# A graph layer with routed experts: first groups of 256 nodes, four row buffers, head steps placed later

## The chip, the cores and the metric

The kernel runs on one core of a Trainium2 chip. A core has a matrix engine (PE, with its weight loads shown apart as PEld), a vector engine (DVE), a scalar engine (ACT), a general engine (POOL, which here makes the descriptors of indirect transfers) and a queue engine (SP, which here issues the plain transfers). Each engine runs its own instructions strictly in the order in which they were written and waits at semaphores for the others. The metric is the device time of one execution in microseconds (us), given as the median of several runs.

## The reference

One layer over 6250 nodes of 256 features and 200000 edges:

```python
xn = layernorm(x)
# edges: w = sigmoid(relu(xn[dst] @ W1 + b1) @ W2 + b2)
num = segment_sum(xn[dst] * w, src); den = segment_sum(w, src)
gnn = where(den > 0, num / max(den, 1e-12), 0)
# heads: 8 heads of 32 channels; k and v are xn normalised per head, kv = k^T v / N
mix = xn @ kv (per head) + xn
x = x + gnn + mix
# experts: softmax of a small router over layernorm(x), the best 2 of 6,
# each expert three 256x256 products with relu between; weighted sum of the two
out = x + experts(layernorm(x))
```

The weight w depends only on the node at the far end of an edge, so it is computed once per node. The indices dst are uneven: low node numbers occur far more often.

## The kernel before, in words

The 6250 nodes are 49 tiles of 128 rows (the last has 106). Two tiles are a block (SB = 2) and four tiles a group (GT = 4); so there are 25 blocks and 13 groups.

**Node rows.** Each node gets a row of three bf16 terms of (w·xn, w, 1), 774 values, which is stored in DRAM (`y_rows`). The first 1024 nodes' rows also stay on the chip (`yh`).

**Sorting.** The edges are cut into pieces of 65536 and sorted by src. Two pieces (a and c) are "cold": for each tile of src nodes, windows of 128 sorted edges are gathered from `y_rows` by an indirect transfer (line 902) and summed by a product with a one-hot matrix (line 933, three matmuls for one gather). There are 1176 such gathers, and we count time by them: "gather 144" is the place in PE's order behind 144 × 3 matmuls of line 933. The third piece (b) is "hot": it holds only dst below 768, so its edges are counted into matrices by one-hot products (line 1101, fed by DVE's lines 1092 and 1094) and multiplied with `yh` (line 1120). A remainder of 3392 edges ("few") is gathered at line 526 and added by an indirect transfer into a DRAM table (line 548), whose rows are read back tile by tile (`tb`, line 1112). The sort is a merge network on DVE (lines 263, 278, 279) with transposes on PE (line 308).

**Heads.** `head_squares` (lines 665 to 701) and `heads` (703 to 756) build kv. Per group: two matmuls for the deviations (683), squares on ACT (685), sums by head (690), a square root on ACT (696), two small DVE steps (698, 699); then per pair of tiles four matmuls into `dv` (715), a DVE product `z` (721) and matmuls that accumulate kv (733).

**Experts.** `Work` walks over the groups in two lines of work. `to_sums` adds the heads' output to x (1145), then the hot counts and the cold sums of each block (`hot_sums`, 1107). `to_experts` runs the experts of a group once `before_experts` (layer norm, router, gates) is through: matmuls with 512 moving columns at line 1285 and with 256 at line 1302.

**What sets the order.** All engines' orders are written by a planner in the program. In the sort stage several lines of work are generators that yield a pair (busy, wait) of assumed nanoseconds; `run` resumes whichever is due on an assumed clock, and one gather step is placed after each 4100 assumed ns while the few edges last, then after each 1600. From there on a loop places one gather step, then as much other work as a credit allows: the credit grows by (work left − 150000 ns) / (gather steps left). Its clock `now` goes on by 336 ns per gather step (TERMS × BFNS) and by what the placed work is assumed to take; a step of `before_experts` is placed when that clock has reached its due time. A gather buffer (18 of them) comes free when PE has used it, 10 gathers are issued ahead of the step that uses them, and the tail of 150000 assumed ns is what remains behind the last gather.

Of the kernel before, what the change touches and what calls it, by code (L numbers as in the profile page):

```python
# [17 lines left out]
P = 128  # L18
# [31 lines left out]
def kernel(  # L50
# [614 lines left out]
    def head_squares():  # L665


        def load(g):
            if g < len(groups):
                _, t0, nt, rows, r = groups[g]  # L670
                xts[g] = hw.tile([P, GT, CB, P], FP, name="xt", bufs=3)
                nc.sync.dma_start(xts[g][:, :nt, :, :r], xnT_d[t0 : t0 + nt, :, :, :r].rearrange("t p c n -> p t c n"))

        load(0)
        yield 0, 3000
        for g, t0, nt, rows, r in groups:
            while len(xts) > 2:
                yield 0, 1000
            load(g + 1)
            sqs = []  # L680
            for c in range(CB):
                dev = sq_ps.tile([P, GT * P], FP, name="turn")
                nc.tensor.matmul(dev[:, :rows], centre, xts[g][:, :nt, c, :r], start=True, stop=True)  # L683
                sqs.append(hw.tile([P, GT * P], FP, name=f"sq{c}", bufs=1))
                nc.scalar.activation(sqs[c][:, :rows], dev[:, :rows], AF.Square)
            yield 0, 4000
            sums = sq_ps.tile([P, GT * P], FP, name="turn")[:, : GT * CB * HB4]
            for c in range(CB):
# [7 lines left out]
            nc.scalar.activation(some, sums[:r, : nt * CB * HB4], AF.Sqrt, scale=1.0 / (HC - 1))  # L696
            yield 0, 3000
            nc.vector.tensor_scalar(some, some, EPS, None, op0=ALU.add)
            nc.vector.reciprocal(some, some)
            hsqs[g] = hsq.rearrange("p (t h) -> p t h", h=HB4)  # L700
            yield 300, 0

    def heads():
# [3 lines left out]
        for g, t0, nt, rows, r in groups:  # L707
# [3 lines left out]
            for j0 in range(0, nt, 2):  # L711
                k = min(2, nt - j0)
                for j in range(k):
                    for c in range(CB):
# [1 line left out]
                            dv[:r, (j * CB + c) * P : (j * CB + c + 1) * P], xt[:, j0 + j, c, :r], centre,  # L716
                            start=True, stop=True,
                        )
                yield 0, 2600
                z = zs[j0 // 2]  # L720
                nc.vector.tensor_tensor(
                    z[:r, : k * CB, :P].rearrange("p b (h c) -> p b h c", c=HC),
# [297 lines left out]
        return u, xT  # L1020

    nodes, kept = {}, {}
    last_group = len(groups) - 1

    def load(g):
        _, t0, nt, rows, r = groups[g]
        nodes[g] = node_load(nt, r, x[t0 * P : t0 * P + rows], xnT_d[t0 : t0 + nt])


# [27 lines left out]


    F32NS, BFNS = 1.67, 112.0
    hot_wt = {}  # L1060

    def hot_counts(blk):
# [41 lines left out]
            yield BFNS, 300.0  # L1104
        return cn

    def hot_sums(blk, u):
# [219 lines left out]
    class Work:  # L1327
# [3 lines left out]
        def __init__(self):  # L1331
            self.now, self.due, self.left = 0.0, 0.0, ALL
            self.sums, self.late, self.chain = self.to_sums(), self.to_experts(), []
            self.terms, self.ready, self.begun, self.ended = -1, -1, -1, -1
            self.time, self.landed = [0.0, 0.0], 0.0
            hot_wt[0] = hot_load(0)

        def next_load(self):

# [3 lines left out]
                self.landed = self.now + 10000.0  # L1343

        def to_sums(self):
            for g, (_, t0, nt, rows, r) in enumerate(groups):
# [4 lines left out]
                self.terms = g  # L1351
                self.next_load()
                for blk in range(t0 // SB, -(-(t0 + nt) // SB)):
                    while min(NTILE, (blk + 1) * SB) - 1 not in cold_edges.sums:
                        yield None
                    yield from hot_sums(blk, u)
                while self.ended < g - 2:
                    yield None
                kept[g] = []
                self.chain.append((g, before_experts(u, nt, rows, r, kept[g])))  # L1360

        def to_experts(self):
            for g, (_, t0, nt, rows, r) in enumerate(groups):
                while self.ready < g:
                    yield None

# [5 lines left out]
                    yield took, took * SHARE  # L1372
                self.ended = g

        def spend(self, took):

            self.now += took
            self.left -= took
            while self.chain and self.now >= self.due:
                g, steps = self.chain[0]  # L1380
                try:
                    self.due = self.now + next(steps)
                except StopIteration:
                    self.chain.pop(0)
                    self.ready = g
# [18 lines left out]
    with tc.manual_schedule(engines=ORDERED):  # L1404
        work = Work()
        credit = 0.0
        while cold_edges.done < len(steps_c):
# [15 lines left out]


    bad = const.tile([P, 1], I32, name="bad")
# [127 lines left out]
```

## Time and profile before

| | |
|---|---|
| median of 3 runs | 2050.33 us (2047.11 to 2052.64) |
| profiled execution, its own time | 2332.55 us |
| its span | 2330.6 us |
| granted PE clock, mean | 0.884 |
| busy: PE, DVE, ACT, POOL | 1817.9, 1255.5, 653.1, 1209.0 us |
| gathers of line 902 | 1176, 1127.0 us busy, 958 ns each |

The profiled execution is 282 us longer than the median. A profile is one execution with the recorder on; its parts are compared with each other and with its own time. In a row of waits, "A <- B" says that A stood idle until B was done. "remote" or "another core or an unknown queue" is an event for which the records name no instruction, and "issue" a wait that they don't explain. Busy times of PE are of a pipeline, so a busy PE isn't one at its peak. A matmul of fp32 operands stands as two records in the profile (the heads and the experts), one of bf16 operands as one (lines 933, 1101 and 1120).

### The profile page before, as it was taken

How to read it: one execution, taken by the hardware profiler on the slowest of the kernel's cores; microseconds unless marked ns; L12 is line 12 of the kernel's file. 1: busy time of each engine (PE TensorE's matmuls, PEld its weight loads, DVE VectorE, ACT ScalarE, POOL GpSimd, SP SyncE). 2: the span in 40 equal slices, each digit the busy share in tenths (PEclk: the TensorE clock that was granted, in tenths of full speed). 3: DMA queues.
4: the chain of work that ended last, by engine and by line, in shares of the span. 5: the costliest groups of instructions: out<-in, count | busy, mean ns of one | idle time of the engine just before them, and what ended most of it. 6: DMA issues, size and time to landing. Idle time of an engine off the chain costs nothing.

```text
span 2330.6 us, 30207 instructions
## 1 busy us (share of the span) xinstructions
PE 1817.9 (78%) x9491; PEld 1181.1 (51%) x9491; DVE 1255.5 (54%) x5004; ACT 653.1 (28%) x1438; POOL 1209.0 (52%) x1243
## 2 busy tenths in 40 slices
PE   1663697434566989989889888998989888889997
PEld 0341475323343555555555555555555555556555
DVE  8899565763654646445464445544545445554431
ACT  5674485731011212112121211212112121121332
POOL 0004666646564566666666666666666666663000
PEclk9665798756787999999999999999999999999999
DMA  8744557436444455555555554555555555553000
GB/s 249 213 165 91 116 139 220 130 91 177 119 133 129 126 137 166 142 169 135 137 167 140 168 139 135 164 139 167 139 141 157 142 160 141 140 163 81 15 10 12
DMA packets 163693, 320.57 MB, mean 138 GB/s; under 512 B 31407, under 2 KB 104406, under 8 KB 163526
## 3 DMA queue, kind: packets, MB, share of 16 engines
q0 software_dynamic: 80800, 241.85, 39.1%
q1 hardware_dynamic: 77262, 76.15, 10.6%
q10 hardware_dynamic: 5464, 0.58, 0.3%
q8 instruction: 76, 1.25, 0.2%
q14 instruction: 91, 0.75, 0.1%
HBM read 285.06 MB, written 33.39 MB: 137 GB/s over the span
## 4 chain that ended last, share of the span: by engine, by line
PE 59%; DVE 17%; another core or an unknown queue 8%; issue 7%; ACT 4%; DMA 3%; SPq 1%; POOL 0%; ACTq 0%; DVEq 0%; POOLq 0%
PE px L1285 20%; PE pu L933 14%; PE px L1302 9%; PE ph L1101 4%; PE ph L1120 4%; DVE k_cb L278 2%; DVE k_cb L279 1%; DVE fr L1094 1%; DVE to L1092 1%; DMA xs<-in_x_dram 1%; DVE k_a L278 1%; PE px L1180 1%; PE turn L683 1%; DVE k_a L279 1%
## 5 line engine op out<-in xcount | busy, mean ns | idle before, releaser
L902 POOL DMA_INDIRECT gt<-y_rows,dsts x1176 | 1127.0, 958 | 676.2 <-issue 236.5
L933 PE MATMUL pu<-gt,hot 128*128 128x258 bf16 x3528 | 601.5, 288 | 23.1 <-issue 11.7
L933 PEld LDWEIGHTS <-hot 128*128 128x128 bf16 x3528 | 358.9, 103 | 384.3 <-issue 301.8
L1294 ACT ACTIVATE h<-px,eb_t 128x512 f32<-128x512 f32 (+1 forms) x312 | 205.8, 662 | 546.3 <-PE pu L933 233.2
L1285 PE MATMUL px<-fT,ew_t 128*128 128x512 f32 (+1 forms) x624 | 317.1, 604 | 4.2 <-issue 4.1
L1302 PE MATMUL px<-ew_t,h 128*128 128x256 f32 (+1 forms) x1176 | 309.1, 391 | 3.2 <-ACT h L1294 1.6
L1285 PE MATMUL px<-h,ew_t 128*128 128x512 f32 (+1 forms) x624 | 304.7, 583 | 1.7 <-issue 1.6
L1094 DVE TENSOR_SCALAR fr<-count,rdl 128x128 bf16<-128x128 bf16 x884 | 227.8, 273 | 88.8 <-PE ph L1101 40.7
L1311 DVE SCALAR_TENSOR_TENSOR acc<-px,gate,acc 128x256 f32<-128x256 f32 (+1 forms) x294 | 128.4, 477 | 265.8 <-PE px L1302 128.6
L916 DVE TENSOR_SCALAR hot<-count,loc 128x128 bf16<-128x128 bf16 x1056 | 238.9, 269 | 52.1 <-PE pu L933 25.6
L1101 PE MATMUL ph<-to,fr 128*128 128x256 bf16 x884 | 191.2, 287 | 77.1 <-DVE fr L1094 33.8
L1302 PEld LDWEIGHTS px<-ew_t,h 128*128 128x128 f32 (+1 forms) x1176 | 210.5, 196 | 34.7 <-issue 10.1
L1092 DVE TENSOR_SCALAR to<-count,hloc 128x256 bf16<-128x256 bf16 x612 | 183.5, 302 | 31.4 <-PE ph L1101 19.6
L1120 PE MATMUL ph<-yh,cn 128*128 128x258 bf16 x882 | 139.4, 283 | 34.3 <-issue 16.4
L1103 ACT CAST cn<-ph 128x256 bf16<-128x256 f32 x150 | 54.6, 373 | 362.0 <-PE ph L1101 191.1
L1101 PEld LDWEIGHTS <-fr 128*128 128x128 bf16 x884 | 88.6, 100 | 113.0 <-DVE fr L1094 53.8
L526 POOL DMA_INDIRECT gt<-y_rows,dst_c x27 | 30.4, 1127 | 198.4 <-DVE k_a L279 190.5
L1120 PEld LDWEIGHTS <-cn 128*128 128x128 bf16 x882 | 88.1, 100 | 63.4 <-issue 48.4
L1285 PEld LDWEIGHTS px<-fT,ew_t 128*128 128x128 f32 x624 | 102.1, 202 | 28.6 <-issue 20.5
L1285 PEld LDWEIGHTS px<-h,ew_t 128*128 128x128 f32 x624 | 98.3, 194 | 31.6 <-issue 27.2
L1130 DVE TENSOR_TENSOR cs<-ph,cs 128x258 f32<-128x258 f32 x49 | 20.9, 427 | 149.3 <-PE pu L933 66.2
L1148 DVE TENSOR_TENSOR u<-ph,u 128x256 f32<-128x256 f32 (+1 forms) x49 | 20.3, 421 | 105.8 <-PE pu L933 40.8
(239 smaller groups left out, 1818.8 us busy)
## 6 DMA issues: line engine op xcount, KB each, us to landing
gt<-y_rows,dsts POOLq DMA_INDIRECT x1176
xs<-in_x_dram SPq DMA_DIRECT2D x24, 512.0 KB
y_rows<-ys SPq DMA_DIRECT2D x10, 774.0 KB
table<-zero SPq DMA_DIRECT2D x50, 129.0 KB
tb<-table SPq DMA_DIRECT2D x49, 129.0 KB
xnT_d<-xnT SPq DMA_DIRECT2D x12, 512.0 KB
xt<-xnT_d SPq DMA_DIRECT2D x12, 512.0 KB
u<-in_x_dram SPq DMA_DIRECT2D x12, 512.0 KB
```

What stands on the lines that cost most here:

```text
L278: nc.vector.tensor_tensor(lo, a, b, op=ALU.min)
L902: nc.gpsimd.indirect_dma_start(out=gt.rearrange("p k w -> p (k w)"), out_offset=None, in_=y_rows, in_offset=bass.IndirectOffsetOnAxis(ap=d ...
L916: nc.vector.tensor_scalar(hot1, count[:, half * P : (half + 1) * P], loc[:, j : j + 1], None, op0=ALU.is_equal)
L933: nc.tensor.matmul(self.pu, hot1, gt[:, k], start=(start and k == 0), stop=(stop and k == TERMS - 1))
L1092: nc.vector.tensor_scalar(made[j1], count, loc[:, j1 : j1 + 1], None, op0=ALU.is_equal)
L1094: nc.vector.tensor_scalar(fr, count[:, :P], rdl[:, d1, j1 : j1 + 1], None, op0=ALU.is_equal)
L1101: nc.tensor.matmul(pa, matrices[i], made[j], start=(j == j0), stop=(j == j1 - 1))
L1120: nc.tensor.matmul(pu[:, :W], cn[:, d, s * P : (s + 1) * P], yh[:, d, k], start=(d == 0 and k == 0), stop=(d == HOT - 1 and k == TERMS - 1),)
L1285: nc.tensor.matmul(ph[:, :rows], w[:, e, c, f * P : (f + 1) * P], ins[:, c, :rows], start=(c == 0), stop=(c == CB - 1),)
L1294: nc.scalar.activation(h[:, f, :rows], ph[:, :rows], AF.Relu, bias=bc)
L1302: nc.tensor.matmul(po[:r, j - j0], h2[:, c, j * P : j * P + r], ew_t[2][:, e, c, :], start=(c == 0), stop=(c == CB - 1),)
L1311: nc.vector.scalar_tensor_tensor(acc[:r, j, :], po[:r, j - j0], gate[:r, j, e : e + 1], acc[:r, j, :], op0=ALU.mult, op1=ALU.add)
```

## The change

1. Three assumed waits of the heads' generators grow by 2000 ns each (4000 to 6000, 3000 to 5000, 2600 to 4600), so that later steps stand further behind what they read.
2. The expert groups are no longer the groups of the earlier stages: the first four tiles make two groups of two tiles, then follow groups of four; 14 groups in place of 13.
3. The rows of the table (`tb`) get four buffers in place of two.
4. The planner's clock goes on where no work could be placed: by GATHER − 336 = 914 ns per gather step that found none, and by 100 ns where the loop couldn't step. Such time isn't taken from the work that is left (`filled`).
5. The first block's hot counts wait for ten gather steps after the loop's begin (`listed`).

```diff
-            yield 0, 4000
+            yield 0, 6000
...
-            yield 0, 3000
+            yield 0, 5000
...
-                yield 0, 2600
+                yield 0, 4600
...
+    def expert_groups():
+        t0 = 0
+        while t0 < NTILE:
+            nt = min(SB if t0 < GT else GT, NTILE - t0)
+            rows = min(nt * P, N - t0 * P)
...
+            yield t0, nt, rows, min(P, rows)
+            t0 += nt
...
+    GATHER = 1250.0
...
-        tbs = {t: op1.tile([P, W], FP, name="tb") for t in tiles}
+        tbs = {t: op1.tile([P, W], FP, name="tb", bufs=4) for t in tiles}
...
-            add_sums(u[:, t % GT], cs, t, r)
+            add_sums(u[:, t - t0], cs, t, r)
...
+            self.listed = cold_edges.done + 10
...
-                    while min(NTILE, (blk + 1) * SB) - 1 not in cold_edges.sums:
+                    while min(NTILE, (blk + 1) * SB) - 1 not in cold_edges.sums or cold_edges.done < self.listed:
...
-        def spend(self, took):
+        def spend(self, took, filled=True):
             self.now += took
-            self.left -= took
+            self.left -= took * filled
...
             else:
                 credit = max(credit, 1000.0)
+                work.spend(100.0, False)
             while credit > 0:
                 took = work.step()
                 if took is None:
+                    work.spend(GATHER - TERMS * BFNS, False)
                     credit = 0.0
                     break
...
             if work.step() is None:
-                work.spend(500.0)
+                work.spend(500.0, False)
```

What it does to the order, read from both programs' instruction lists, where each matmul counts once: the heads' last matmul (733) stands at gather 64 in place of 30; the sort's last transpose at gather 119 in place of 116; the first expert matmul at gather 174 in place of 222. The hot counts begin at gather 144 in both. Between gathers 144 and 288 stand 96 expert matmuls of 256 columns (line 1285) in place of 36 of 512, 48 of line 1302 in place of 24, and 156 of line 1120 in place of 180; between 288 and the last gather 428 in place of 440 of line 1285, 414 in place of 440 of line 1302, and 672 in place of 648 of line 1120. Behind the last gather the work is the same but for two matmuls of line 1302.

More of the change, by code (lines that the diff above doesn't have):

```diff
@@ L1022 @@
     nodes, kept = {}, {}
-    last_group = len(groups) - 1
+    def expert_groups():
[3 more added lines that the diff above has]
+            rows = min(nt * P, N - t0 * P)
+            assert rows % P == 0 or nt == 1, "the rows that don't fill a tile make a group of their own"
+            yield t0, nt, rows, min(P, rows)
+            t0 += nt
+    parts = list(expert_groups())
+    last_group = len(parts) - 1
     def load(g):
-        _, t0, nt, rows, r = groups[g]
+        t0, nt, rows, r = parts[g]
         nodes[g] = node_load(nt, r, x[t0 * P : t0 * P + rows], xnT_d[t0 : t0 + nt])
@@ L1105, in hot_counts, with hot_sums @@
         return cn
-    def hot_sums(blk, u):
+    def hot_sums(blk, u, t0):
         tiles = range(blk * SB, min(NTILE, (blk + 1) * SB))
-        tbs = {t: op1.tile([P, W], FP, name="tb") for t in tiles}
+        tbs = {t: op1.tile([P, W], FP, name="tb", bufs=4) for t in tiles}
         for t, tb in tbs.items():
@@ L1345, in to_sums @@
         def to_sums(self):
-            for g, (_, t0, nt, rows, r) in enumerate(groups):
+            for g, (t0, nt, rows, r) in enumerate(parts):
                 while g not in nodes or self.now < self.landed:
@@ L1353, in to_sums @@
                 for blk in range(t0 // SB, -(-(t0 + nt) // SB)):
-                    while min(NTILE, (blk + 1) * SB) - 1 not in cold_edges.sums:
+                    while min(NTILE, (blk + 1) * SB) - 1 not in cold_edges.sums or cold_edges.done < self.listed:
                         yield None
-                    yield from hot_sums(blk, u)
+                    yield from hot_sums(blk, u, t0)
                 while self.ended < g - 2:
@@ L1362, in to_experts @@
         def to_experts(self):
-            for g, (_, t0, nt, rows, r) in enumerate(groups):
+            for g, (t0, nt, rows, r) in enumerate(parts):
                 while self.ready < g:
```

## The prediction

> **What bounds the kernel now.** I cut the span at events of the trace: the first and the last `z` of the heads (246.3 and 396.1 us), the last step of the sort (555.5), gather 144 (591.0), gather 288 (834.3), and the last gather's matmul (2144.5). In the table of stretches the columns are length, busy time of PE, PEld, DVE, ACT and POOL, granted PE clock, share of DMA, GB/s.
>
> ```profile
> 246.30:396.10 149.80, 117.26 (x781) 96.75 (x780) 77.67 (x155) 90.07 (x246) 92.56 (x78) 0.86 0.65 167
> 396.10:555.50 159.40, 70.71 (x395) 50.35 (x394) 101.56 (x216) 82.75 (x230) 93.86 (x93) 0.68 0.44 120
> ...
> 591.00:834.30 243.30, 173.75 (x998) 110.66 (x996) 128.60 (x636) 33.86 (x75) 135.83 (x143) 0.83 0.47 128
> 834.30:2144.50 1310.20, 1161.60 (x6182) 738.66 (x6181) 656.88 (x3076) 250.26 (x486) 827.17 (x871) 0.95 0.54 148
> 2144.50:2330.60 186.10, 169.86 (x679) 107.05 (x677) 57.52 (x211) 55.48 (x103) 0.00 (x0) 0.96 0.04 12
> ```
>
> I call them stages 1 to 5 (1 heads, 2 sort, 3 early blocks, 4 steady part, 5 tail). Stage 4 is PE's: 1161.6 of 1310.2 us busy, at 1.475 us per gather. Stage 3 has fewer experts and yet 1.69 us per gather (243.3 / 144), with PE idle for 69.5 us. Next, who stands in whose way: POOL's waits from stage 3 to 4, then PE's own time line in stage 3.
>
> ```profile
> POOL gt L902 <- issue: 202.5, 646, 1.1
> POOL gt L902 <- PE pu L933: 172.3, 171, 3.2
> POOL gt L902 <- PE ph L1101: 100.5, 94, 6.3
> ```
>
> ```profile
> 605.17 4.84 PE L933 MATMUL pu<-gt,hot 128*128 128x258 bf16 x42
> 609.95 0.24 PE L829 MATMUL pT<-ident,wt_a 24*128 24x24 f32 x1
> 610.12 0.51 PE L933 MATMUL pu<-gt,hot 128*128 128x258 bf16 x3
> 624.91 0.30 PE L829 MATMUL pT<-ident,wt_b 25*128 25x25 f32 x1 [14.28 <-issue]
> ```
>
> An unhindered gather takes 0.95 us and 0.30 us to the next, so 1.25. "issue" is that pause; the other two rows, 273 us, are POOL standing until PE gives a buffer back. The time line has the reverse: PE eats 14 stored gathers in 4.84 us, then stands 14.3 us while POOL issues one per 1.25 us. Both sides wait by turns, so uneven work costs time.
>
> In stages 1 and 2 the chain that ended last runs through DVE's sort steps, PE's head matmuls and transposes. DVE's waits in stage 1:
>
> ```profile
> DVE z L721 <- PE dv L715: 35.0, 12, 9.4
> DVE hsq L698 <- ACT hsq L696: 16.3, 6, 5.2
> DVE z L721 <- remote: 7.5, 1, 7.5
> ```
>
> DVE is idle for 72.1 of 149.8 us, mostly at a `z` or a root that isn't ready, and the sort's steps stand behind it in its order. Prices come from these groups (count, busy, mean ns):
>
> ```profile
> L902 POOL DMA_INDIRECT gt<-y_rows,dsts x1176 | 1127.0, 958 | 676.2 <-issue 236.5 <-PE pu L933 219.5 <-PE ph L1101 100.5
> L1285 PE MATMUL px<-fT,ew_t 128*128 128x512 f32 x576 | 310.7, 631 | 4.2 <-issue 4.1
> L1302 PE MATMUL px<-ew_t,h 128*128 128x256 f32 x1152 | 303.1, 391 | 3.2 <-ACT h L1294 1.6 <-issue 1.3
> L1285 PE MATMUL px<-h,ew_t 128*128 128x512 f32 x576 | 298.4, 609 | 1.7 <-issue 1.6
> L278 DVE TENSOR_TENSOR k_cb<-k_cb 128x512 f32<-128x512 f32 x90 | 61.6, 684 | 10.0 <-ACT k_cb L309 8.3
> ```
>
> The means hold pauses between unlike instructions; in the tail's unbroken runs 16 records of line 1285 take 6.87 us and 16 of line 1302 take 3.45. So a program's matmul (two records) costs 0.86 us of 512 columns and 0.43 of 256 in a run, 1.24 and 0.78 by the means.
>
> **Part 1, the heads' waits.** No instruction is added, but between the first and the last `z` now stand 138 sort steps in place of 92 (58 in place of 37 pairs of lines 278 and 279), and behind the last one 126 in place of 176. Those 50 steps took from 396.5 to 444.6 us in the trace: 48 us go from stage 2, with the scalar engine's counts and PE's transposes around them. Stage 1 gets 42 × 0.684 us and 4 × 0.445 us = 30.5 us of DVE work. If all of it lies in DVE's 72 us of waits, stage 1 stays as long; if none does, it grows by 30.5 and 17 us remain. But PE's order also brings 34 more gathers into stage 1 (64 for 30): POOL had 92.6 us busy and 78 pauses of 0.30 = 116 us, and 34 × 1.25 = 42 make 158, over the 149.8. So the gain is 17 to 40 us. Less head work in front of the few edges' matmuls helps (PE was busy for 117 us). Moved past on SP: the load of the first group's x now stands in front of the last five loads of `xt`, and it waited 16.3 us for the table's scatters; PE's later head matmuls would stand behind it once. I take **28 us**.
>
> A rule stands against it. The Trainium skill (SBUF — State Buffer, on the shared port pair and its "DVE blocks DMA" trap) says that POOL is locked out of the port for descriptors while DVE runs a copy, cast or tensor_scalar in a two-port mode, so that denser DVE work starves gathers. The rows: a gather took 1.02 us between 400 and 530 us with the sort (74.52 us, 73 of them), 0.94 in the steady part. By the row, 34 moved gathers cost 34 × 0.08 = 3 us, inside the 28; by the rule's worst case each waits a whole 0.68 us step, 23 us, and 5 us of the gain remain. The sort steps are two-input operations that page excepts for writes, so I take the row.
>
> **Part 2, groups of two tiles and the planner's clock.** Stage 3 gets 96 half-width matmuls of line 1285 for 36 full ones: 96 × 0.43 − 36 × 0.86 = +10.6 us (by the means 96 × 0.78 − 36 × 1.24 = +30.4); 24 more of line 1302, +10.4 (+18.8); 24 fewer of line 1120, at 0.115 us in runs, −2.8 (−6.8 by their 283 ns). Together +18 us (+42). PE's idle 69.5 us covers both. Does the stage shorten as well? The hot counts, packed into few gathers while no expert work was ready, now alternate with it from gather 174, not 222. At stage 4's busy share (0.887), 192 us of PE work take 216 us, a gain of 27; by the means 216 us take 243, none. POOL's floor, 144 × 1.25 = 180, doesn't bind. I take **14 us**.
>
> Here a second rule speaks against: The Trainium skill (TensorE: Matmul & The Clock Gate, "Why this matters for your kernels") advises against moving sides under 512, as thin products let the clock fall to half. The runs of line 1302 show half the time for half the columns (0.216 to 0.429 us per record), its mean in mixed order 0.62 of it. That is the difference between 27 and none above; the granted clock of stage 3, 0.83, would rise if the gaps fill. I lean to the runs.
>
> Stage 4 loses 12 matmuls of line 1285, 26 of line 1302 and gains 24 of line 1120: −10.3 − 11.2 + 2.8 = −19 us (−28 by the means, 0 if gathers paced it). PE sets the pace there: **19 us**. The second small group adds a router, gates and two table loads of 1.28 us on ACT, which is idle for 210 us of stage 3, and two transfers on SP; nothing.
>
> **Part 3, four `tb` buffers, `listed`, idle clock.** SP stood 431.8 us for line 1129 of DVE at the read of `tb`, with the windows of edges and x queued behind. But those windows are fetched a block ahead, and from 600 us on PE waited for them only 4.2 us; its "keys" waits are starved gathers as above. Zero, within 0 to 4. The hot counts start at gather 144 in both, so `listed` moves nothing. The tail has two matmuls more, 0.9 us.
>
> **Sum.** 2332.55 − 28 − 14 − 19 + 1 = 2272.5 us for a profiled execution, a ratio of 0.9743. The median is 282 us lower and I can't say in which stage; in proportion, 2050.33 × 0.9743 = **1998 us**.
>
> **Rivals** (savings times 0.879, the ratio of median to profiled time).
> Every cover holds: 40 + 27 + 28 = 95 us, **1967 us**. For it: PE idle in stage 3 and DVE in stage 1; against: POOL's 158 us.
> Only the sort gains and the later stages are paced by gathers: 17 us, **2035 us**. For it: POOL's 273 us of waits show both near the limit; against: PE busy 0.887.
> Slower: `z` waits longer. Its matmuls now stand behind 64 / 25 = 2.6 gather steps per `z` in place of 1.2, in PE's order; where gathers are late, `z` waits, and behind it the whole sort on DVE. The waits named above, 50 us with two small ones, are 2.0 us each. From 2.4 us more per `z` the 61 us are gone; the 1.4 steps at stage 2's 1.77 us are 2.5. At 3.5 us more, 87 − 61 = +26 us, **2073 us**. Against it: 2.6 steps also give PE's and ACT's results more time.
> Nothing moves: the early work only fills gaps that later gathers reopen, **2050 us**.
>
> **How the numbers follow.** Chances: forecast 0.42 (own range 1982 to 2016: 39 to 78 us in place of the 60, times 0.879), full cover 0.15, sort alone 0.20, slower 0.18, nothing 0.05. A measurement of this kernel can tell about 0.3% (6 us) from no change. Faster by more: 0.42 + 0.15 + 0.17 of the third = 0.74; within: 0.03 + 0.05 + 0.01 = 0.09; slower: 0.17. The range from 1958 to 2062 holds the first three and part of the fourth.
>
> **What would show it.** Right: the sort ends 20 to 40 us earlier than 555.5 with `z` waiting less; gathers 144 to 288 take 216 to 235 us, PE's clock above 0.83; gathers 288 to 1176 about 1290 us; the tail 186 again. Wrong: stage 1 longer by as much as stage 2 is shorter, `z` waiting over 4 us each, or stage 4 unchanged at 1.475 us per gather, with POOL no longer waiting for PE.

## The result, and the profile after

The changed kernel takes 2054.75 us (median of 20 runs, 2047.89 to 2059.32), the kernel before in the same session 2047.37 us (20 runs, 2039.76 to 2053.38): a ratio of 1.0039, 95% interval [1.0026, 1.0051]. The change costs some 8 us where a saving of 52 was forecast. The time lies inside the forecast's range, on the wrong side of no change.

On one of the four chips that the experiments ran on every version takes 2321 to 2334 us, on the other three the kernel before takes 2048; the profile that the prediction was made from (2332.55 us) fits that one chip, and the timed runs fit the others. So the first experiment was to profile the kernel before once more.

> The kernel before, unchanged, profiled once more. If its first profile (2330.6 us) shows what the timed executions do, the span is 2300 to 2350 us again and gathers 288 to 1176 take 1.475 us each. If that profile held stalls that the timed executions don't have (my reading of why the changed kernel's profile is 2057.5 us and its median only 2054.75), the span is 2040 to 2060 us, that stretch takes 1.24 us a gather with PE over 95% busy, and the early blocks (gathers 144 to 288) take some 205 us in place of 243.

It took 2051.01 us, span 2049.0, so the second theory held (1.253 us per gather in stage 4, stage 3 at 194 us). The table of stretches of the kernel before on this chip, cut at the same events (first and last `z`, sort end, gathers 144 and 288, last gather), with the columns length, busy PE, PEld, DVE, ACT, POOL, granted PE clock, share of DMA, GB/s:

```profile
248.90:388.20 139.30, 112.52 (x782) 94.28 (x780) 78.12 (x155) 90.08 (x246) 92.37 (x78) 0.88 0.69 176
388.20:528.80 140.60, 62.83 (x382) 47.43 (x381) 101.56 (x218) 82.42 (x230) 85.51 (x84) 0.71 0.46 126
...
556.30:750.50 194.20, 168.20 (x997) 107.34 (x996) 128.44 (x642) 34.28 (x76) 146.46 (x154) 0.91 0.63 170
750.50:1862.80 1112.30, 1088.98 (x6183) 719.70 (x6182) 654.87 (x3074) 254.57 (x484) 831.15 (x873) 1.00 0.64 174
1862.80:2049.00 186.20, 169.90 (x679) 107.07 (x676) 57.48 (x211) 55.54 (x103) 0.00 (x0) 0.96 0.04 12
```

And the changed kernel, cut in the same way (its profiled execution took 2059.32 us, the longest of its 20, span 2057.5):

```profile
249.80:437.00 187.20, 132.17 (x902) 110.25 (x903) 107.14 (x204) 125.93 (x354) 124.02 (x112) 0.83 0.64 169
437.00:536.40 99.40, 44.59 (x259) 32.47 (x258) 70.68 (x170) 43.39 (x120) 51.02 (x51) 0.68 0.38 105
...
563.30:770.70 207.40, 185.46 (x1161) 136.68 (x1160) 135.79 (x678) 48.70 (x115) 148.28 (x155) 0.90 0.59 166
770.70:1870.10 1099.40, 1071.88 (x6123) 707.35 (x6121) 650.90 (x3069) 249.36 (x478) 828.69 (x871) 1.00 0.63 176
1870.10:2057.50 187.40, 171.13 (x684) 108.19 (x681) 57.95 (x211) 55.58 (x103) 0.00 (x0) 0.97 0.04 12
```

Two things are to be seen. The 282 us between the first profile and the runs are 49 of stage 3, 198 of stage 4 and 29 of stages 1 and 2 together, with 5 elsewhere: stage 4 is 1.253 us per gather here (1112.30 / 888), not 1.475. And of the change: stage 1 is 48 us longer, stage 2 only 41 shorter, stage 3 is 13 longer and stage 4 13 shorter, so that these two together are as long as before (1306.5 and 1306.8).

POOL's waits from gather 144 to the last, before and then after, tell what sets the pace of stages 3 and 4 (waiting for what, us in total, times, longest). In the changed kernel the lines named here stand 12 further down: 1101 is 1113, 1285 is 1297.

```profile
POOL gt L902 <- issue: 146.0, 479, 0.3
POOL gt L902 <- PE pu L933: 68.4, 224, 0.5
POOL gt L902 <- PE ph L1101: 43.3, 135, 1.4
```

```profile
POOL gt L902 <- issue: 146.5, 481, 0.3
POOL gt L902 <- PE pu L933: 74.1, 217, 3.7
POOL gt L902 <- PE ph L1113: 46.6, 135, 4.3
```

Before, nearly every wait is the 0.30 us that lie between any two gathers, whatever is named as its releaser: 68.4 / 224 = 0.305. POOL hardly ever stands for PE (the longest such wait is 1.4 us). It takes 0.95 + 0.30 = 1.25 us for each gather, and that paces the kernel, though PE, 98% busy in stage 4, has little room left. From the starts of the gathers in the trace, gathers 144 to 1175 are issued in 1299.6 us, only 11 us more than 1031 × 1.25. (In the first profile it is 1564.7, 276 us more.) After the change single waits of 3.7 and 4.3 us have come in.

So each span is a sum of three: the time at which gather 144 is issued, the issue of the other 1031, and what is left after the last one.

| run | gather 144 issued | 144 to last issued | last issued to end | span |
|---|---|---|---|---|
| before, again | 548.1 | 1299.6 | 201.3 | 2049.0 |
| after | 555.7 | 1309.4 | 192.4 | 2057.5 |
| heads_only | 561.1 | 1302.7 | 199.7 | 2063.5 |
| clock_only | 545.6 | 1296.3 | 192.8 | 2034.7 |
| after_old_heads | 548.5 | 1305.3 | 191.1 | 2044.9 |

The changed kernel loses 7.6 us up to gather 144 and 9.8 behind it, and gains 8.9 after the last gather. Each row is one execution: the profiled ones of after_old_heads and clock_only are 5 us shorter than the medians of their runs, that of the changed kernel 5 us longer, so differences of a few us between rows can be chance. The experiments say which part did which.

### The profile page after: what moved, and what is told of

It is laid out like the page before. It is cut to its first block, busy times and chain, and to the rows that moved or that the text cites. A ratio compares the mean times of both kernels' runs of the same rounds, so it can differ in the third digit from the quotient of the medians.

```text
span 2057.5 us, 30457 instructions
## 1 busy us (share of the span) xinstructions
PE 1736.6 (84%) x9591; PEld 1173.4 (57%) x9591; DVE 1255.7 (61%) x5036; ACT 664.7 (32%) x1471; POOL 1212.3 (59%) x1243
## 4 chain that ended last, share of the span: by engine, by line
PE 63%; DVE 10%; DMA 5%; issue 2%; ACT 2%; POOL 1%; SPq 0%; ACTq 0%; DVEq 0%; POOLq 0%
PE px L1297 22%; PE pu L933 16%; PE px L1314 11%; PE ph L1132 5%; PE ph L1113 4%; DMA gt<-y_rows,dsts 4%; DVE fr L1106 1%; PE ph L1157 1%; PE px L1192 1%; POOL gt L902 1%; DVE to L1104 1%; DVE k_cb L278 1%; DVE k_cb L279 1%; DMA table<-sm,few_row 1%; PE px L1185 1%
## 5 line engine op out<-in xcount | busy, mean ns | idle before, releaser
L933 PE MATMUL pu<-gt,hot 128*128 128x258 bf16 x3528 | 583.2, 281 | 38.5 <-DMA gt<-y_rows,dsts 36.2
L933 PEld LDWEIGHTS <-hot 128*128 128x128 bf16 x3528 | 350.4, 101 | 355.5 <-issue 272.5
L1306 ACT ACTIVATE h<-px,eb_t 128x512 f32<-128x512 f32 (+2 forms) x336 | 212.4, 633 | 519.4 <-PE px L1297 514.5
L1297 PE MATMUL px<-fT,ew_t 128*128 128x512 f32 (+2 forms) x672 | 301.7, 545 | 0.6 <-ACT fT L1186 0.6
L1297 PE MATMUL px<-h,ew_t 128*128 128x512 f32 (+2 forms) x672 | 301.0, 543 | 0.0
L1314 PE MATMUL px<-ew_t,h 128*128 128x256 f32 (+1 forms) x1176 | 297.1, 381 | 0.0
L1314 PEld LDWEIGHTS px<-ew_t,h 128*128 128x128 f32 (+1 forms) x1176 | 204.7, 190 | 25.4 <-issue 4.3
L526 POOL DMA_INDIRECT gt<-y_rows,dst_c x27 | 37.5, 1387 | 199.8 <-DVE k_a L279 191.9
L1297 PEld LDWEIGHTS px<-h,ew_t 128*128 128x128 f32 x672 | 104.6, 192 | 24.6 <-issue 19.2
L1297 PEld LDWEIGHTS px<-fT,ew_t 128*128 128x128 f32 x672 | 104.1, 191 | 24.2 <-issue 15.4
L278 DVE TENSOR_TENSOR k_cb<-k_cb 128x512 f32<-128x512 f32 (+1 forms) x99 | 65.5, 662 | 17.3 <-ACT k_cb L309 15.3
```

Of the source, the lines that this page charges most:

```text
L278: nc.vector.tensor_tensor(lo, a, b, op=ALU.min)
L933: nc.tensor.matmul(self.pu, hot1, gt[:, k], start=(start and k == 0), stop=(stop and k == TERMS - 1))
L1297: nc.tensor.matmul(ph[:, :rows], w[:, e, c, f * P : (f + 1) * P], ins[:, c, :rows], start=(c == 0), stop=(c == CB - 1),)
L1306: nc.scalar.activation(h[:, f, :rows], ph[:, :rows], AF.Relu, bias=bc)
L1314: nc.tensor.matmul(po[:r, j - j0], h2[:, c, j * P : j * P + r], ew_t[2][:, e, c, :], start=(c == 0), stop=(c == CB - 1),)
```

## The experiments

### One part at a time

**heads_only** is the kernel before with the three longer waits of the heads:

```diff
-            yield 0, 4000
+            yield 0, 6000
...
-            yield 0, 3000
+            yield 0, 5000
...
-                yield 0, 2600
+                yield 0, 4600
```

> Only the three longer waits in the heads' generators. The theory of the prediction (sort steps fill DVE's waits): 15 to 28 us faster, ratio 0.987 to 0.993. The rival (the sort ends earlier by some 20 us, but gathers or the wait of DVE for the few edges' scatters give it back): 0 to 5 us either way, 0.998 to 1.002. The rival that this part is what costs: 5 to 15 us slower, 1.003 to 1.007.

Measured 2063.9 us, ratio 1.0067 [1.0043, 1.009], against 2049.36 of the kernel before in that session: 14 us lost, as the third theory had it.

**clock_only** is the kernel before with the planner's clock alone, groups of 512 as they were:

```diff
+    GATHER = 1250.0
...
+                work.spend(100.0, False)
...
+                    work.spend(GATHER - TERMS * BFNS, False)
...
-                work.spend(500.0)
+                work.spend(500.0, False)
```

> Only the planner's clock that goes on while nothing could be placed; groups of 512 as before. If earlier expert work fills idle PE time: 5 to 20 us faster, 0.990 to 0.998. If the early blocks aren't idle in timed executions: 0.999 to 1.003.

Measured 2041.33 us, ratio 0.9961 [0.9949, 0.9973]: 8 us gained. Of the 14 us between the two profiles 8.5 lie after the last gather (201.3 to 192.8 us in the table). The first expert matmul stands at gather 202 in place of 222, and PE is less far behind POOL when the gathers end: it is through with the last one 7.9 us after its issue in place of 15.4.

**after_old_heads** is the changed kernel with the heads' old waits. The groups were not run without the new clock. The run also has the four `tb` buffers and `listed`; it is read here as groups and clock, though what the buffers do alone wasn't measured.

> The changed kernel with the heads' old waits (groups of 256 first, the idle clock, four row buffers). If the loss of 8 us against the kernel before comes from the groups and the heads' part saves: 1.008 to 1.015. If it comes from the heads' part: 0.995 to 1.000. If the parts are both near nothing: 1.001 to 1.004.

Measured 2051.24 us, ratio 1.0003 [0.9991, 1.0015]. Beside clock_only the groups of 256 cost 8.6 us ((1.0003 − 0.9961) × 2048). Between this and the whole change the heads cost 7 us ((1.0039 − 1.0003) × 2048), alone 14: the parts don't add up exactly, and the intervals leave some 5 us to either side. The run fell between the three ranges that had been set down for it.

### What the heads' waits ran into

In the changed kernel's order of time, DVE stands once in the middle of stage 1, and so do ACT and SP's queue (start, length, engine, line, what it stood for):

```profile
339.43 0.68 DVE L721 TENSOR_TENSOR z<-dv,hsq 128x512 f32<-128x512 f32 x1
362.96 0.31 DVE L996 CAST ident_b<-ident 128x128 bf16<-128x128 f32 x1 [22.85 <-DMA table<-sm,few_row]
```

```profile
365.45 0.40 ACT L913 ACTIVATE away<-count,loc 128x128 bf16<-128x128 bf16 x1 [25.70 <-DMA u<-in_x_dram]
```

```profile
362.68 0.38 SPq L1017 DMA_DIRECT2D u<-in_x_dram  x1
363.11 0.46 SPq L1019 DMA_DIRECT2D xT<-xnT_d  x1
363.61 0.47 SPq L1004 DMA_DIRECT2D ew_t<-in_L_ffn_expert_w_dram  x1
364.12 1.06 SPq L672 DMA_DIRECT2D xt<-xnT_d  x1
```

DVE's waits in stage 1 of the kernel before, for comparison:

```profile
DVE z L721 <- PE dv L715: 36.4, 15, 8.9
DVE ident_b L996 <- issue: 9.6, 1, 9.6
```

`ident_b`, the experts' constants, their weights and the first x take the memory of the pool that the few edges used, so all of them wait for the last scatter into the table, issued at 359 us. Before, DVE came to it at 352 us and stood 9.6; with the longer waits it stands 16.9 (heads_only) and 22.9 us (after, from 340 on). The size varies: it is 5.8 us in clock_only and was 2.7 in the first profile, with the same order in that stage. On SP a load of `xt` stands behind the loads of x and weights. The waits of DVE and of PE in stage 1 of the changed kernel:

```profile
DVE z L721 <- PE dv L715: 28.3, 10, 8.8
DVE ident_b L996 <- DMA table<-sm,few_row: 22.9, 1, 22.9
```

```profile
PE turn L683 <- DMA xt<-xnT_d: 23.6, 2, 20.7
```

Whether this stop is the loss can be tested by moving what waits.

**heads_late_consts** and **heads_late_both** write the constants, and in the second the first load of x too, behind the sort's last loop:

```diff
-        load(0)
         while any(a.open for a in beside):
...
         piece_sorted(cold[1])
+        load(0)
+    rw1_t = wp.tile([P, CB, P], FP, name="rw1_t")
...
+    nc.vector.tensor_copy(ident_b, ident)
```

> The heads' longer waits alone, and with them the experts' small constants (their loads on the scalar engine's queue, the casts of eb3 and ident_b on DVE) written behind the sort stage's last loop instead of ahead of it. With the heads alone DVE stood 16.9 us at ident_b and ACT 20.3 us near its loads, both until the last scatter of the few edges, whose pool's memory the constants take over. Theory 'a stop behind the scatters' (the moved steps find their cover, and the loss is the stop that they now stand behind): 10 to 20 us less than the heads alone, so 2044 to 2054 us, ratio 0.997 to 1.002. Theory 'no cover' (stage 1 is paced elsewhere and the moved steps only lengthen it): within 5 us of the heads alone, ratio 1.004 to 1.009.

> As heads_late_consts, and the first load of x and xT for the experts is issued behind the loop too, so that no later load of xt stands behind it on SP's queue. With the heads alone PE waited 24.4 us for xt, 23.3 of them once. Theory 'a stop behind the scatters': 20 to 28 us less than the heads alone, 2036 to 2044 us, ratio 0.993 to 0.998, with the wait for xt under 5 us and stage 1 at 165 to 172 us in place of 191. Theory 'no cover': stage 1 stays above 180 us, ratio 1.002 or more. If only SP's queue counts and not DVE's stop, this one gains and heads_late_consts doesn't.

Measured 2060.15 us, 1.0064 [1.0048, 1.008], and 2057.11 us, 1.0047 [1.003, 1.0065]. They tell little, since the edit missed: `ident_b` stood where it had, since it was written outside the ordered part of the program, and DVE still waited 16.3 us for it in heads_late_both. PE still waited 16.5 us once for `xt`, behind the weights on SP.

**clock_late_both**, the same edit on clock_only:

> The planner's clock alone, which was 0.9961 of before, with the same two late placements and the old waits of the heads. Theory 'a stop behind the scatters': the kernel before has this stop too, at 9.6 us of DVE, so 4 to 10 us less than the clock alone, ratio 0.991 to 0.994. Theory 'no cover': the same as the clock alone, 0.995 to 0.997.

Measured 2037.1 us, 0.9948 [0.9935, 0.996]. It is the lowest ratio on the faster chips, but its interval overlaps that of clock_only, and DVE stands 5.8 us at `ident_b` in both.

**heads_behind**, **clock_behind** and **clock_heads_behind** have all of it in the ordered part, behind the loop: the constants, the 18 weight loads, then the load of x.

```diff
-    line_w = Line(expert_loads())
-    beside = [line_w, line_u[1], line_q, line_h, line_b, line_u[2], line_e]
+    beside = [line_u[1], line_q, line_h, line_b, line_u[2], line_e]
...
         piece_sorted(cold[1])
+        rw1_t = wp.tile([P, CB, P], FP, name="rw1_t")
...
+        nc.vector.tensor_copy(ident_b, ident)
...
+        for _ in expert_loads():
+            pass
+        load(0)
```

> The heads' longer waits alone, and now truly behind the sort stage's last loop: the experts' constants, the 18 loads of the experts' weights and the first load of x. In the two earlier tries the constants' instructions kept their places (DVE still stood 16.3 us at ident_b), because the scheduler puts what is written outside an ordered part as early as it can; only the load of x had moved, and the weight loads in front of it in SP's queue still waited for the scatters. Here ident_b stands behind the last z on DVE. Theory 'a stop behind the scatters': 17 us of DVE and 17 of PE at xt go, 15 to 25 us less than the heads alone, 2038 to 2048 us, ratio 0.995 to 1.000. Theory 'no cover': stage 1 stays above 180 us and the ratio at 1.003 to 1.007, with new waits at z or at the gathers in place of those that went.

> The planner's clock alone with the heads' old waits, and the same things behind the loop. The stop of the kernel before is 9.6 us of DVE, so theory 'a stop behind the scatters' expects 5 to 10 us less than the clock alone, ratio 0.991 to 0.994; theory 'no cover' 0.995 to 0.997.

> The planner's clock, the heads' longer waits, and the same things behind the loop. If the longer waits are good once the stop is gone, this is the fastest, 0.987 to 0.991. If they cost by themselves, it lies above the clock with the same things behind the loop, by 3 to 10 us, at 0.994 to 1.000.

Measured 2056.98 us, 1.0037 [1.0024, 1.0049]; 2040.23 us, 0.9957 [0.9941, 0.9974]; 2043.71 us, 0.9983 [0.9969, 0.9997]. Now the stop is gone. Stages 1 and 2 of heads_behind, and then of clock_behind, which has the old waits:

```profile
248.30:412.20 163.90, 134.15 (x902) 112.63 (x903) 106.13 (x198) 126.23 (x354) 118.05 (x105) 0.86 0.62 152
412.20:512.10 99.90, 44.91 (x254) 32.02 (x252) 71.14 (x170) 43.41 (x120) 56.52 (x57) 0.67 0.44 115
```

```profile
244.90:367.20 122.30, 108.06 (x778) 90.79 (x779) 75.86 (x149) 89.88 (x246) 80.00 (x67) 0.92 0.59 143
367.20:508.90 141.70, 64.43 (x380) 47.77 (x379) 101.59 (x218) 82.40 (x230) 94.57 (x93) 0.70 0.49 132
```

Together 263.8 and 264.0 us: the longer waits make stage 1 41.6 us longer and stage 2 41.8 shorter. With the stop it was 290.5 in heads_only and 279.9 before. So in this sum, one profile of each, the longer waits cost 11 us with the stop, and without it they are worth nothing. What the move brings to the two stages, 27 us with the longer waits and 14 with the old ones (277.7 in clock_only), is lost again at once. The waits of heads_behind between the sort's end and gather 144:

```profile
DVE u L1149 <- PE ph L1146: 26.6, 3, 25.5
PEld ph L1146 <- DMA xT<-xnT_d: 25.6, 1, 25.6
PE ph L1146 <- DMA xT<-xnT_d: 25.1, 1, 25.1
POOL gt L902 <- PE pu L933: 12.4, 4, 11.3
```

`xT` is queued behind 18 weight loads, PE stands 25 us for it, its gather buffers fill up and POOL stops. The longer waits still cost 5 us on top of the clock here (0.9983 against 0.9957, intervals that overlap a little), and heads_behind 8 against before; of the 14 us of heads_only the move took back 6. Where these 5 to 8 us lie isn't settled: the late xT is in all three, and the single profiles differ by 3 us ahead of the first gather alone. By their ratios heads_behind and clock_behind fall to the theory 'no cover', and clock_heads_behind to the longer waits costing by themselves; but stage 1 of heads_behind fell to 163.9 us, where 'no cover' had it above 180.

### On the slower chip

The next version has neither the stop nor the late xT: the loads begin once the last `z` is placed, x first.

```diff
     def expert_loads():
+        load(0)
+        rw1_t = wp.tile([P, CB, P], FP, name="rw1_t")
...
-                yield 0, 4000
+                yield 0, 2500
...
-    line_w = Line(expert_loads())
+    line_w = Line(expert_loads(), [line_h])
...
-        load(0)
         while any(a.open for a in beside):
```

> The kernel before, with its old waits; what writes into the few edges' memory (the first load of x, the experts' constants, their 18 weight loads) is placed once the last z is placed, and no longer ahead of it or behind the whole loop. The tries behind the loop shortened z to sort end to 264 us in place of 280 (290 with the longer waits), and lost that again at gather 120 to 144, where PE stood 25 us for xT, whose load was queued behind the 18 weight loads. Theory 'a stop behind the scatters': the 16 us of the sort stay, ratio 0.991 to 0.995. Theory 'the gathers pace it anyway' (POOL needs 1.25 us per gather and gather 144 comes no earlier): ratio 0.998 to 1.001.

> The heads' longer waits alone with the same placement. Theory 'the stop is the whole loss and the moved steps are worth nothing': within 3 us of the old waits with this placement. Theory 'the longer waits cost by themselves': 5 to 8 us above it. The forecast's own theory (the moved steps find cover once nothing stops DVE): 10 to 28 us below it.

> The planner's clock alone (0.9961) with this placement and the old waits of the heads. Theory 'a stop behind the scatters': 16 us less than the clock alone, ratio 0.986 to 0.990, the fastest of all. Theory 'the gathers pace it anyway': 0.995 to 0.997.

> The whole change with this placement. Theory 'the stop is the whole loss of the heads': it comes to the old waits with this placement, the clock's 8 us less and the groups' 8.6 us more, so within 4 us of it, ratio 0.990 to 0.996. Theory 'the longer waits cost by themselves': 0.997 to 1.001.

> The planner's clock with the placement behind the last z, once more: the chip of the last four runs takes 2329 us for the kernel before, where the others took 2048, so that their ratios hold for that chip alone. On a chip at 2048 us: theory 'a stop behind the scatters' 0.986 to 0.990 (z to sort end 264 us in place of 280, and gather 144 14 us earlier); theory 'the gathers pace it anyway' 0.994 to 0.997. From gather 144 on no version can be shorter than 1032 x 1.25 = 1290 us, since POOL issues one gather per 1.25 us.

> The same with the heads' longer waits, so that the two differ in these waits alone and neither has the stop or the late xT. Theory 'the stop is the whole loss and the moved steps are worth nothing': within 3 us of the other one. 'The longer waits cost by themselves': 5 to 8 us above it. The forecast's own theory (28 us of cover): 10 to 28 us below it.

All six ran on the chip where the kernel before takes 2329 to 2331 us; the last two were meant for a faster one.

| run | us | ratio |
|---|---|---|
| before_after_z | 2333.73 | 1.0004 [0.9984, 1.0025] |
| heads_after_z | 2325.23 | 0.9979 [0.9961, 0.9997] |
| clock_after_z | 2326.93 | 0.9979 [0.9963, 0.9996] |
| clock_after_z_2 | 2325.87 | 0.9972 [0.9955, 0.999] |
| clock_heads_after_z | 2320.81 | 0.9948 [0.9929, 0.9966] |
| change_after_z | 2331.5 | 1.0017 [0.9996, 1.0038] |

There the longer waits, without the stop, gain 6 us (0.9979 against 1.0004) and 6 to 7 on top of the clock (0.9948 against 0.9972 and 0.9979); each pair of intervals overlaps a little, but the sign is the same in all three comparisons. From the first z to the sort's end heads_after_z takes 301.5 us and before_after_z 309.0, so some of the cover is there on this chip. The groups, with four `tb` buffers and `listed`, cost 16 us there (1.0017 against 0.9948), and the whole change missed both ranges set down for it. The gain expected from the placement itself didn't come: gather 144 is issued at 563.8 us in before_after_z, as in the first profile. The stretch where clock_behind was fast, gathers 60 to 118 in 96.2 us where the kernel before takes 107.3, takes 115.1 in before_after_z and 109.8 in the first profile; why is open. What the placement would do on a faster chip wasn't measured.

### What the groups of 256 ran into

The stops of POOL can be placed. In clock_only no gather after 144 comes more than 0.35 us later than 1.25 us behind the one before; in after_old_heads gathers 300 to 304 do, by 10.8 us in all, and in the changed kernel by 12.0 at the same gathers (elsewhere single ones, by 1.1 us at most). POOL's order of time in the changed kernel there:

```profile
751.28 0.95 POOL L902 DMA_INDIRECT gt<-y_rows,dsts  x1 [0.30 <-issue]
754.66 0.95 POOL L902 DMA_INDIRECT gt<-y_rows,dsts  x1 [2.43 <-PE pu L933]
759.88 0.94 POOL L902 DMA_INDIRECT gt<-y_rows,dsts  x1 [4.27 <-PE ph L1113]
764.57 0.97 POOL L902 DMA_INDIRECT gt<-y_rows,dsts  x1 [3.75 <-PE pu L933]
```

Gather 300 needs the buffer of gather 282, 18 earlier. PE at that place:

```profile
753.05 1.00 PE L1113 MATMUL ph<-to,fr 128*128 128x256 bf16 x3 [0.24 <-DVE fr L1106]
753.89 0.50 PE L933 MATMUL pu<-gt,hot 128*128 128x258 bf16 x3
755.30 2.35 PE L1113 MATMUL ph<-to,fr 128*128 128x256 bf16 x6 [0.91 <-DVE fr L1106]
758.56 0.40 PE L1113 MATMUL ph<-to,fr 128*128 128x256 bf16 x1 [0.92 <-DVE fr L1106]
758.75 0.85 PE L933 MATMUL pu<-gt,hot 128*128 128x258 bf16 x3
759.40 1.49 PE L1113 MATMUL ph<-to,fr 128*128 128x256 bf16 x6
763.25 0.40 PE L1113 MATMUL ph<-to,fr 128*128 128x256 bf16 x1 [2.37 <-DVE fr L1106]
763.44 0.85 PE L933 MATMUL pu<-gt,hot 128*128 128x258 bf16 x3
```

Between two gather steps stand seven or eight hot counts and no expert matmul, PE waits for DVE to make their operands, and three gather steps in a row take 4.1 to 4.9 us. In clock_only at most two hot counts stand between gather steps there. This is the packed counting of stage 3 once more: the small groups left it there (gathers 144 to 148 and 168 to 172 still have six to eight counts each) and added a place of it.

Two runs put the split elsewhere, on the new clock and with two `tb` buffers and no `listed`: **clock_split_mid** splits three groups in the steady part, **clock_split_second** the second one.

```diff
-            nt = min(SB if t0 < GT else GT, NTILE - t0)
+            nt = min(SB if 4 * GT <= t0 < 7 * GT else GT, NTILE - t0)
```

```diff
-            nt = min(SB if t0 < GT else GT, NTILE - t0)
+            nt = min(SB if GT <= t0 < 2 * GT else GT, NTILE - t0)
```

> The planner's clock, and three of the groups of 512 nodes (tiles 16 to 27) split into six of 256, in the steady part where PE is busy 98% of the time; the first group stays whole. The one group split ahead cost 8.6 us over the clock alone (1.0003 against 0.9961). Theory 'half-width matmuls cost more than half': each split costs the same wherever it lies, 3 x 6 to 10 = 18 to 30 us over the clock alone, ratio 1.005 to 1.011. Theory 'the place is the cost' (starved gathers in the early blocks, which early experts take PE from): a split in the steady part costs 0 to 3 us, ratio 0.996 to 1.001.

> The planner's clock, and only the second group (tiles 4 to 7) split into two of 256. The order up to gather 260 is that of the clock alone, and the half-width matmuls stand between gathers 260 and 400. Three splits in the middle cost 3.1 us each. Theory 'the early place is the cost': 3 us over the clock alone, ratio 0.997 to 0.9985. Theory 'any split near the early blocks costs what the first one does': 8 us, ratio 0.9995 to 1.001.

Measured 2048.79 us, 1.0005 [0.9994, 1.0016], and 2044.01 us, 0.9975 [0.9964, 0.9985]. Over clock_only that is 9.0 us for three splits, 3.0 each, and 2.9 for one at the second group; the first group's costs 8.6. So a split elsewhere costs about 3 us for its half-width matmuls and what comes with a group, and the other 6 go to the place at the first group. The single profiles agree on where: the three splits lengthen what is left after the last gather (201.2 us for 192.8), the first group's split lengthens gathers 144 to the last (1305.3 for 1296.3) and nothing behind them. What a group brings with it besides the width wasn't taken apart.

## Why the prediction was wrong

Three steps of the sum failed. The 19 us of stage 4 took PE for what sets the pace, and it is POOL; the 14 us of stage 3 covered PE work with idle time that the timed runs don't have; the 28 us of the heads took DVE's waits for free cover. Of these 61 us, Part 2 came as nothing (the clock gained 8, the groups lost 8.6) and Part 1 as a loss of 7 to 14. That the time lies inside the range is luck, since the range took in a rival of the wrong mechanism.

**The base.** The sum was made against one execution that doesn't stand for the runs. "I can't say in which stage" was true, and "in proportion" was the choice that carried it. The 69.5 us of PE idle in stage 3, the 1.475 us per gather and POOL's 273 us of waits for PE, on which Part 2 rests, aren't there in the second profile, which is as long as the timed runs: 26.0 us, 1.253 and next to none. (Of the 273, some 80 us were in any case the pause of 0.30 us, 265 times.) The warning stood in the text: an unhindered gather takes 1.25 us, and gather 144 at 591.0, 1031 more at 1.25 and the tail of 186.1 make 2066, near the median. I had the floor and didn't ask whether the runs stand on it.

**Part 2, stage 4, −19 us.** PE was taken for the bound. Here it is POOL, at 1.25 us per gather, so PE work taken out of stage 4 can only shorten what is left after the last gather: 201.3 to 191.1 us, 10 us, and the clock alone gets 8.5 of them. It is what a rival had ("the later stages are paced by gathers"), against which I put PE busy 0.887.

**Part 2, stage 3, −14 us.** With 26 us of idle time no gain was to be had: 207.4 for 194.2 us, of which stage 4 gives 13 back. "Alternate with it from gather 174" counted what left the early packing and not where the counts would pile up next: at gathers 282 to 285, for 11 to 12 us of POOL. (96 × 0.43 − 36 × 0.86 is +10.3, not +10.6; nothing hangs on it.)

**The price of half-width products.** By the trace's unbroken runs a half-width matmul is half the price, by the means 0.62, and I leaned to the runs. The means here are 382 to 397 ns for 256 columns and 594 to 599 for 512, 0.64 to 0.67 again. The granted clock hardly moved: 0.90 in stage 3 for 0.91, and 1.00 in stage 4 in both. (The Trainium skill, TensorE: Matmul & The Clock Gate, "Why this matters for your kernels", warns of a clock that goes up and down for products of M under 512 that wait for transfers between their parts; that isn't what was changed here, and no run here shows it.) In the rows below (columns after the count: busy us, mean ns), the 192 records of half width are busy 57.1 us, where 96 of full width take 48.4 (96 × 532.9 / 1056). The price by measurement, about 3 us for a split, lies between that difference of 8.7 and the nothing that I leaned to.

```profile
L1297 PE MATMUL px<-fT,ew_t 128*128 128x512 f32 x528 | 267.8, 599 | 0.6 <-ACT fT L1186 0.6
L1297 PE MATMUL px<-h,ew_t 128*128 128x512 f32 x528 | 265.1, 594 | 0.0
...
L1297 PE MATMUL px<-h,ew_t 128*128 128x256 f32 x96 | 29.6, 397 | 0.0
L1297 PE MATMUL px<-fT,ew_t 128*128 128x256 f32 x96 | 27.5, 382 | 0.0
```

**Part 1, −28 us.** The step that failed is the cover: "if all of it lies in DVE's 72 us of waits, stage 1 stays as long; if none does, it grows by 30.5". It grew by 41.6 without any stop, more than DVE's own 30 us, and stage 2 shrank by as much (clock_behind against heads_behind). So the moved steps found no cover on this chip. The chain that ended last (the work followed back from the last instruction, step by step, to what it waited for) shows where they went. The shares of stage 1 by line, cut off after the largest, in clock_behind and then in heads_behind, one execution each:

```profile
by line: PE ph L733 17.7%; PE dv L715 16.2%; PE turn L683 14.4%; PE turn L690 14.3%; DMA table<-sm,few_row 8.6%; PE pu L933 6.6%; issue 5.6%; DVE z L721 4.0%; PE turn L308 3.3%; PE pT L543 3.2%; DMA gt<-y_rows,dsts 2.6%; ACT junk L371 1.2%;
by line: DVE k_cb L278 12.5%; DVE k_cb L279 11.6%; ACT junk L371 10.2%; PE ph L733 6.5%; PE turn L690 6.2%; PE dv L715 6.1%; PE turn L683 5.6%; issue 5.5%; DMA gt<-y_rows,dsts 4.5%; PE pu L933 4.5%; DMA xt<-xnT_d 3.3%; DVE z L721 3.0%; DMA 
```

With the old waits the heads' four lines of PE hold 63% of the chain and the sort's lines on DVE are not among its largest; with the longer ones those four hold 24% and the sort's two lines 24%. The steps stand on the chain, not under it. Why they can't be covered stays open. PE has 124 more matmul records there, 26 us (134.15 for 108.06), but its busy share falls from 88% to 82%. POOL has 36 more gathers of line 902 (73 for 37), 45 us at 1.25 each, about what the stage grew by, as the prediction's own 34 × 1.25 = 42 had warned; but it hardly waits for PE, and PE waits only 13.6 us for gathers. No run isolates either.

**The slower rival** had the right sign and the wrong mechanism: `z` waits 28.3 us in 10 waits after the change against 36.4 in 15 before. The stop was in my text as "PE's later head matmuls would stand behind it once", for 16.3 us of SP, and costed at nothing beside the gain. DVE's `ident_b` and ACT's constants, which wait for the same scatter and stand in the same place of the order, aren't in it: the sum went through the queues that a step is moved past, and a wait for memory isn't in the diff. That the stop is what the heads lose is shown for 11 us in the profiles; the timed runs took back only 6 of 14 when it was moved, with a late `xT` in its place.

**The rule on the port.** The worst case that I had worked out from the rule of The Trainium skill (SBUF — State Buffer, "DVE blocks DMA"), 23 us, didn't come: a gather in stage 1 took 1.003 us with more sort steps (79 of them, 79.22 us) and 1.043 before (46, 47.98 us). It is no test of the rule, since DVE's busy share of the stage stayed at 56 to 57% as the stage grew; the 3 us that I allowed weren't there either.

**What held.** The tail at 186 (187.4). The four `tb` buffers and `listed` at nothing weren't tested alone. The sort's end 20 to 40 us earlier did not hold (536.4 for 528.8, 7.6 later). "Wrong: stage 1 longer by as much as stage 2 is shorter" is what came, once the stop was gone.

## What to carry to other kernels

Before a sum is made, hold the profiled execution against the runs; where they are 12% apart, find the floor of the pacing engine (here 0.95 + 0.30 us per gather) and see which of the two it fits. A step that is placed later in an in-order engine runs into whatever stands there, and that includes constants and loads which wait only because their memory was another stage's: look for the first instructions that write into reused memory. Where a producer runs a fixed number of buffers ahead (18 here), it isn't only the mean load that counts: four packed steps in a row stopped it for 11 to 12 us.

## What the runs showed of the hardware

**One chip of four was slower.** The kernel before takes 2048 us on three chips and 2329 to 2331 on a fourth, in both sessions there (106 runs of 2315 to 2348 us). All six profiles from that chip issue gathers 144 to the last in 1556 to 1564 us, as the first profile does (1565), where the other chips' take 1296 to 1319. The gathers' own times are alike (1127 us for 1176 in the first profile, 1132 in the second), and so is the tail (186.1 and 186.2). The time goes where PE, DVE and POOL hand work to each other: in the first profile PE is busy 89% of stage 4 in place of 98%, POOL stops some 205 us, and the granted clock is 0.95 in place of 1.00. What begins it stayed open. A change's worth needn't be the same on both: the longer waits without the stop gain about 6 us there and cost about 5 here, both near the edge of the intervals.

**The granted clock goes with PE's busy share** in these tables: 1.00 in stage 4 on the faster chips, with PE busy 98% in products of mixed width; 0.90 and 0.91 in stage 3 with 89 and 87%; 0.83 and 0.88 in stage 1 with 71 and 81%; 0.68 and 0.71 in stage 2 with 45% in both.
